# An attention and feed-forward kernel on one core: last product of a projection step behind the unit's values, output bias by column groups and added a unit later

## The chip, the core and the metric

The kernel runs on one core of a Trainium2 chip. The metric is the device time of one execution in microseconds (us). The time before is the median of three runs, 1138.49 us (1137.04 to 1140.65). The engines of a core work side by side, each through its own queue in order: TensorE (PE; its weight loads are shown as PEld), VectorE (DVE), ScalarE (ACT), GpSimd (POOL) and SyncE (SP, which here only issues transfers). Products land in PSUM, from which VectorE and ScalarE read.

## The reference

Four sequences of 1024 tokens with 512 features. First cross attention with 16 heads of 32 features (`_layernorm` subtracts the mean and divides by the deviation), then a feed-forward part whose inputs and weights are rounded to 8-bit steps:

```python
x = x + xattn(layernorm(x), ctx)       # 16 heads, mask below
x = x + ffn(layernorm(x))

# xattn
qh = heads(q @ Wq + bq);  kh = heads(kv @ Wk + bk);  vh = heads(kv @ Wv + bv)
scores = where(mask, qh @ kh.T / sqrt(32), -inf)
out = merge(softmax(scores) @ vh) @ Wo + bo
# mask: tokens 0..767 attend within their own third of 256;
#       tokens 768..1023 attend to 0..767 and causally to each other

# ffn; fq is a rounding to 8-bit steps with one scale for a whole tensor, fw with one for a row
h = fq(silu(fq(x) @ fw(w_gate).T) * (fq(x) @ fw(w_up).T))
return h @ fw(w_down).T
```

The biases bq, bk, bv and bo are not zero.

## The kernel before

The time falls into the attention part (to about 880 us), which this change touches, and the feed-forward part.

**Blocks and units.** Tokens come in 16 blocks of 256, four to a sequence. Three blocks of a sequence attend to their own keys only, the fourth (TEXT) to the keys of all four. A unit is one block of queries, one group of four heads (four groups) and one block of keys; there are 112 units. All products are 32-bit. The values, the sums and the projections go through `column_groups` or its like: four matmuls of 128 rows by 32 columns side by side. One such matmul instruction appears as two records in the trace.

**The loop over units** (lines 819 to 898) writes the order of TensorE, VectorE, ScalarE and GpSimd by hand (`manual_schedule`); SyncE's queue is ordered by the scheduler. A turn n does, in this order:

1. `maxima` of unit n: scores s, reduced on VectorE to row maxima.
2. Perhaps one step of a background task (statistics or normalisation of a block of x, rounding of a weight for the feed-forward part).
3. `large(n)`: one large step. This is a projection step (`big_step`, `run_big`: pp_kv or pp_q through `rows`, or pv) or a step of the output product (`step_output`, `Output.step`: po). A counter `spent` against `target(n)` paces the projections; `outputs` is the queue of finished blocks.
4. What `later` holds from the turn before: quotients of finished units, `add_bias`.
5. `weights` of unit n - 5: scores again, transposed, into t; ScalarE takes their exponentials into pT (two instructions of 128x1024); GpSimd adds these into sp for the softmax sums (L516).
6. `values` of unit n - 6: av, and, at the last key block of a group, the sums (L548, a product of ones with sp).
7. Where the projections are behind, a second large step.

**A projection step.** `rows` makes two halves of 256 columns (`parts`) in one PSUM tile. For each half it adds four products over the input chunks (`ci`); each product is one call of `column_groups`. After both halves ScalarE takes them out with bias and scale (line 286). A pv step fills 512 columns and ScalarE copies them out (line 326). For the last units, from `LATE` on, each step does one half only and has a PSUM tile of its own. A po step is taken out by VectorE, which adds it to xr (line 589).

**PSUM.** `ps_sc` holds three buffers of two banks for s and t; `ps_av` one bank for av; `ps_mm` one bank for all large steps, so each large step waits until the one before is taken out. Before the loop, `bank` uses `ps_sc` for them.

**The output bias.** bo + bv Wo is the same for all tokens. `output_bias` spreads bv over 128 columns (turn 2), multiplies it with Wo in four full matmuls (turn 4) and adds bo on VectorE. `Output.load` loads the block of x into xr; `add_bias` adds bo_b to it on GpSimd (line 584) in the turn after the load.

## Time and profile before

| | |
|---|---|
| median of three runs | 1138.49 us |
| profiled execution, its own time | 1139.15 us |
| its span, first to last instruction | 1137.4 us |
| mean granted TensorE clock | 0.992 |
| TensorE busy | 1116.0 us, 98% |
| VectorE, ScalarE, GpSimd busy | 784.9, 500.1, 551.5 us |
| attention's first part, 0 to 126 us: TensorE busy | 123.9 us |
| steady part, 126 to 740 us: TensorE busy | 612.2 of 614 us |
| late part, 740 to 880 us: TensorE busy | 135.8 of 140 us |

The page sums an engine's busy time over the whole span. A matmul's end in the trace is modelled, and a wait of TensorE shorter than that end isn't seen as idle: it shows in the distance from one start to the next. In a timeline, each row gives the start, the length, the engine, the line, what is written from what, and, in brackets, the idle time before it and what ended that.

### The profile page before, as it was taken

The numbers are of one execution on the slowest core, as the hardware profiler recorded it, in microseconds if no ns is written. First come the engines' busy times: TensorE is split into PE (matmuls) and PEld (weight loads), VectorE is DVE, ScalarE is ACT, GpSimd is POOL, SyncE is SP. The second block draws the span as 40 slices with busy tenths as digits, with TensorE's granted clock in tenths as the row PEclk, the third lists the DMA queues.
The fourth block names the chain that finished last, engine by engine and source line by source line (L and its number), as shares of the span: only waits on it lengthen the run. The fifth ranks groups of instructions, "written<-read, shape, count | busy, mean of one in ns | idle before, by whom it ended". The sixth has DMA issues, their size and how long they took to land.

```text
span 1137.4 us, 31369 instructions
## 1 busy us (share of the span) xinstructions
PE 1116.0 (98%) x13811; PEld 562.5 (49%) x13833; DVE 784.9 (69%) x979; ACT 500.1 (44%) x700; POOL 551.5 (48%) x618
## 2 busy tenths in 40 slices
PE   9999999999999999999999999998999899998998
PEld 5545545455545445454545455555554344444344
DVE  2545776766577857567777765875667788877887
ACT  3234433343444424344433445543333465553553
POOL 1224556577664567775556568657753222110110
PEclk9999999999999999999999999999999899999999
DMA  8342213133222222331312122111311599320895
GB/s 260 109 123 74 62 43 108 47 88 93 80 62 76 79 84 63 95 101 34 92 67 73 56 76 73 37 49 27 106 61 62 164 291 268 69 38 28 290 386 194
DMA packets 117201, 119.09 MB, mean 105 GB/s; under 512 B 55548, under 2 KB 86536, under 8 KB 115656
## 3 DMA queue, kind: packets, MB, share of 16 engines
q1 hardware_dynamic: 111104, 83.26, 26.3%
q0 software_dynamic: 5648, 33.30, 7.6%
q8 instruction: 108, 1.77, 0.7%
q10 hardware_dynamic: 312, 0.53, 0.2%
q14 instruction: 29, 0.24, 0.1%
HBM read 71.57 MB, written 33.29 MB: 92 GB/s over the span
## 4 chain that ended last, share of the span: by engine, by line
PE 91%; DVE 3%; DMA 2%; POOL 2%; ACT 1%; issue 1%; DVEq 0%; POOLq 0%; ACTq 0%
PE pv L219 10%; PE po L219 9%; PE pp_kv L219 9%; PE pp_q L219 9%; PE av L530 9%; PE t L491 8%; PE pg L1045 7%; PE pu L1045 7%; PE s L439 6%; PE s L428 5%; PE t L486 3%; PE av L548 3%; PE pd L1148 2%; DMA xt<-x_d 2%; POOL sp L516 2%
## 5 line engine op out<-in xcount | busy, mean ns | idle before, releaser
L496 ACT ACTIVATE pT<-t 128x1024 f32<-128x1024 f32 x224 | 217.1, 1021 | 190.2 <-PE t L491 160.1
L516 POOL TENSOR_TENSOR sp<-sp,pT 128x1024 f32<-128x1024 f32 x86 | 191.7, 2229 | 39.1 <-ACT pT L496 35.6
L450 DVE TENSOR_REDUCE nmh<-s 128x2 f32<-128x1024 f32 (+1 forms) x128 | 145.3, 1156 | 67.3 <-PE s L439 65.1
L516 POOL TENSOR_TENSOR sp<-pT 128x1024 f32<-128x1024 f32 x59 | 139.9, 2372 | 87.9 <-ACT pT L496 87.7
L432 DVE TENSOR_REDUCE nmh<-s 128x4 f32<-128x1024 f32 x96 | 112.8, 1216 | 97.7 <-PE s L428 95.5
L219 PE MATMUL pp_q<-qT,Wq_sb 128*32 128x256 f32 x2048 | 119.3, 383 | 0.0
L530 PE MATMUL av<-pT,va 128*32 128x256 f32 (+1 forms) x1792 | 116.5, 377 | 1.0 <-ACT avs L893 1.0
L219 PE MATMUL pv<-Wv_sb,kvT 128*32 128x512 f32 (+1 forms) x1088 | 116.9, 570 | 0.0
L491 PE MATMUL t<-qT,kT 32*128 32x256 f32 (+1 forms) x1792 | 113.4, 367 | 0.0
L219 PE MATMUL po<-Wo_sb,oT 128*32 128x512 f32 (+1 forms) x1120 | 110.3, 534 | 0.3
L563 DVE RECIPROCAL avs<-avs 128x256 f32<-128x256 f32 x63 | 109.8, 1742 | 0.0
L219 PE MATMUL pp_kv<-kvT,Wk_sb 128*32 128x256 f32 x1920 | 109.6, 380 | 0.0
L564 POOL TENSOR_TENSOR oT<-avs 128x256 f32<-128x256 f32 x63 | 45.9, 729 | 98.1 <-DVE avs L563 98.0
L491 PEld LDWEIGHTS t<-qT,kT 32*128 32x128 f32 x1792 | 88.3, 185 | 7.0
L1045 PE MATMUL pg<-xqT,wgT 128*128 128x512 bf16 x344 | 90.2, 382 | 1.1 <-DVE xqT L1006 0.5
L1045 PE MATMUL pu<-xqT,wuT 128*128 128x512 bf16 x345 | 90.2, 382 | 0.4
L1051 ACT ACTIVATE silu<-pg,sg 128x512 f32<-128x512 f32 x88 | 60.0, 686 | 65.6 <-PE pg L1045 63.5
L219 PEld LDWEIGHTS pp_q<-qT,Wq_sb 128*32 128x32 f32 x2048 | 63.7, 110 | 48.8 <-issue 8.7
L1072 DVE SCALAR_TENSOR_TENSOR h<-pu,su,silu 128x512 f32<-128x512 f32 x88 | 65.4, 747 | 30.9 <-PE pu L1045 28.3
L219 PEld LDWEIGHTS pp_kv<-kvT,Wk_sb 128*32 128x32 f32 x1920 | 60.1, 110 | 44.1 <-issue 5.4
L439 PE MATMUL s<-kT,qT 32*128 32x256 f32 (+1 forms) x1024 | 76.4, 387 | 3.2 <-ACT pT L496 3.2
L530 PEld LDWEIGHTS av<-pT,va 128*32 128x32 f32 x1792 | 46.8, 109 | 54.5 <-issue 23.7
(186 smaller groups left out, 1387.3 us busy)
## 6 DMA issues: line engine op xcount, KB each, us to landing
xt<-x_d SPq DMA_DIRECT2D x16, 1024.0 KB, 6.4
h<-h_d POOLq DMA_DIRECT2D x3, 2816.0 KB, 13.6
xb<-in_x_dram SPq DMA_DIRECT2D x16, 512.0 KB, 3.7
xr<-in_x_dram SPq DMA_DIRECT2D x16, 512.0 KB, 3.7
x_d<-xr POOLq DMA_DIRECT2D x16, 512.0 KB, 3.9
spread_kv<-in_ctx_dram SPq DMA_DIRECT2D x60, 128.0 KB, 2.7
xn_d<-xb SPq DMA_DIRECT2D x15, 512.0 KB, 3.3
spread_q<-xn_d SPq DMA_DIRECT2D x60, 128.0 KB, 2.7
```

What stands on the lines that cost most here:

```text
L219: nc.tensor.matmul(out[rows_of(j)], lhs[:, rows_of(j)], rhs, start=start, stop=stop, tile_position=(0, j * D), skip_group_check=True)
L432: nc.vector.tensor_reduce(nmh[:, h, :, :, 0], prs[h], AX.X, ALU.max, negate=True)
L439: nc.tensor.matmul(prs[j // 2][:, j % 2, kk, :w], q[rows_of(j), g, i * P : (i + 1) * P], K[k.keys[2 * half + kk]][rows_of(j), g, :w], star ...
L450: nc.vector.tensor_reduce(nmh[:, h, :, i, half], s[:, :, :n], AX.X, ALU.max, negate=True)
L491: nc.tensor.matmul(prs[j // 2][:, j % 2, n, cols], kc[rows_of(j), g, n * P : (n + 1) * P], q[rows_of(j), g, cols], start=False, stop=(n == 1))
L496: nc.scalar.activation(pT[:, 2 * h : 2 * h + 2], prs[h], AF.Exp)
L516: nc.gpsimd.tensor_tensor(sp[:, :, cols], a, pT[:, :, n, cols], ALU.add)
L530: nc.tensor.matmul(av[rows_of(j), 0, cols], va[:, n, g * P + j * D : g * P + (j + 1) * D], u.pT[:, j, n, cols], start=(u.part == 0 and n = ...
L563: nc.vector.reciprocal(avs[:, 1, :], avs[:, 1, :])
L1045: nc.tensor.matmul(ps, w[:, cc, ic * P : (ic + 1) * P], qT[:, cc, :], start=(cc == 0), stop=(cc == NCC - 1))
L1051: nc.scalar.activation(s, pg, AF.Silu, scale=sg[:, ic : ic + 1])
L1072: nc.vector.scalar_tensor_tensor(h[:, ic, :], pu, su[:, ic : ic + 1], s, ALU.mult, ALU.mult)
```

## The change

Three parts.

The last of the products of a large step is held back, with its take: `run_big` and `step` return them as two functions (`rest`), and `complete` runs them. In the loop, `complete` comes straight after the large step where the unit of values in this turn is the last of its group (sums follow), where there is none, where a second large step follows, or where these values need the very block that is being projected. Else it comes after `weights` and `values`. `rows` is rewritten for it: the take of a half now follows the last product of that half, and only the last half's last product and take are held back. In the changed kernel the take of `rows` is line 294.

`add_bias` passes through `later` twice, so it comes one turn later.

The output bias: bv stands in the first of 32 columns with zeros beside it; four matmuls of 128x32, each in its own group of 32 partitions, give four partial products; ScalarE copies them out; a turn later one product with ones adds them up.

```diff
         def output_bias():
-            bvr = wk2.tile([P, NCC, P], F32, tag="wst", name="bvr", bufs=1)
+            bvr = wk2.tile([P, NCC, D], F32, tag="wst", name="bvr", bufs=1)
+            parts = wk2.tile([P, C], F32, tag="sp", name="bo_parts")
             def spread():
-                nc.vector.tensor_copy(bvr, bqk[:, 2 * NCC :].unsqueeze(2).to_broadcast([P, NCC, P]))
+                nc.vector.memset(bvr, 0.0)
+                nc.vector.tensor_copy(bvr[:, :, 0:1], bqk[:, 2 * NCC :].unsqueeze(2))
             def product():
...
-                    nc.tensor.matmul(pb, bvr[:, cc, :], W["Wo"][:, cc, :], start=(cc == 0), stop=(cc == NCC - 1))
+                    nc.tensor.matmul(pb[rows_of(cc)], bvr[:, cc, :], W["Wo"][:, cc, :], start=True, stop=True, tile_position=(0, cc * D), skip_group_check=True)
+                nc.scalar.copy(parts, pb)
+            def total():
+                pb = ps_sc.tile(...)
+                nc.tensor.matmul(pb, ones, parts, start=True, stop=True)
                 nc.vector.tensor_tensor(bo_b, pb, bo_b, ALU.add)
...
             def rows(self, dst, w, b, scale, co, parts):
                 pk = bank(...)
-                for a in parts:
-                    for ci in range(NCC):
-                        lhs = W[w][:, ci, (co + a) * P : (co + a + 1) * P]
-                        column_groups(pk[:, a, :], lhs, self.T[:, ci, :], ci == 0, ci == NCC - 1)
-                for a in parts:
+                def product(a, ci):
+                    lhs = W[w][:, ci, (co + a) * P : (co + a + 1) * P]
+                    column_groups(pk[:, a, :], lhs, self.T[:, ci, :], ci == 0, ci == NCC - 1)
+                def take(a):
                     bias = bqk[:, b + co + a : b + co + a + 1]
                     nc.scalar.activation(dst[:, co + a, :], pk[:, a, :], AF.Identity, bias=bias, scale=scale)
+                todo = [(a, ci) for a in parts for ci in range(NCC)]
+                for a, ci in todo[:-1]:
+                    product(a, ci)
+                    if ci == NCC - 1:
+                        take(a)
+                return (lambda: product(*todo[-1])), (lambda: take(parts[-1]))
...
-                    later.append(self.add_bias)
+                    later.append(lambda: later.append(self.add_bias))
...
+        late_rest = []
+        def finish(rest, rests):
+            late_rest.extend(rest)
+            if not rests:
+                complete()
+        def complete():
+            for f in late_rest:
+                f()
+            late_rest.clear()
...
             full = large(n)
+            v = units[n - V_LAG] if V_LAG <= n < len(units) else None
+            second = n < LATE and spent + BIG < target(n)
+            if v is None or second or v.part == v.parts - 1 or (jobs[at_big - 1].kind, jobs[at_big - 1].c) == ("kv", v.k.keys[v.part]):
+                complete()
...
                 ends = values_now()
                 weights_now()
+            complete()
```

The pv step and `Output.step` are split in the same way: all products but the last at once, the last one and its take in `rest`. With the take of a block's last po step, the load of the next xr moves too. `large` passes `rests=True` to every step it makes; the other callers complete at once.

More of the change, by code (lines that the diff above doesn't have):

```diff
@@ L197, in product @@
                 for cc in range(NCC):
-                    nc.tensor.matmul(pb, bvr[:, cc, :], W["Wo"][:, cc, :], start=(cc == 0), stop=(cc == NCC - 1))
+                    nc.tensor.matmul(pb[rows_of(cc)], bvr[:, cc, :], W["Wo"][:, cc, :], start=True, stop=True, tile_position=(0, cc * D), skip_group_check=True)
+                nc.scalar.copy(parts, pb)
+            def total():
+                pb = ps_sc.tile([P, 2, 2, QB], F32, tag="sc", name="pbt").rearrange("p a b c -> p a (b c)")[:, 0, :]
+                nc.tensor.matmul(pb, ones, parts, start=True, stop=True)
                 nc.vector.tensor_tensor(bo_b, pb, bo_b, ALU.add)
-            return spread, product
+            return spread, product, total
         nc.gpsimd.memset(mask, 0.0)
@@ L312, in run_big @@
                         Q[c] = qp.tile([P, NCC, QB], F32, tag="qT", name=f"qT_{c}")
-                    self.rows(Q[c], "Wq", 0, QK_SCALE, 2 * i, parts)
+                    rest = self.rows(Q[c], "Wq", 0, QK_SCALE, 2 * i, parts)
                 elif i < 2:
@@ L316, in run_big @@
                         K[c] = kp.tile([P, NCC, QB], F32, tag="kT", name=f"kT_{c}")
-                    self.rows(K[c], "Wk", NCC, 1.0, 2 * i, parts)
+                    rest = self.rows(K[c], "Wk", NCC, 1.0, 2 * i, parts)
                 else:
@@ L323, in run_big, with product @@
                     pv = bank(f"pv_{c}_{i}_{parts[0]}")
-                    for ci in range(NCC):
+                    def product(ci):
                         column_groups(pv[:, cols], self.T[:, ci, i * P : (i + 1) * P], W["Wv"][:, ci, cols], ci == 0, ci == NCC - 1)
-                    nc.scalar.copy(V[c][:, i, cols], pv[:, cols])
+                    for ci in range(NCC - 1):
+                        product(ci)
+                    rest = (lambda: product(NCC - 1)), (lambda: nc.scalar.copy(V[c][:, i, cols], pv[:, cols]))
                 if parts[-1] == 1:
@@ L331, in run_big @@
                     self.part = 1
-                return len(parts)
+                return len(parts), rest
         background = deque()
@@ L608, in step, with product, take @@
                 po = ps_mm.tile([P, 512], F32, tag="mm", name=f"po_{self.k.n}_{i}_{self.part}")
-                for cc in range(NCC):
+                last = cols.stop == C
+                def product(cc):
                     column_groups(po[:, cols], self.k.oT[:, cc, i * P : (i + 1) * P], W["Wo"][:, cc, cols], cc == 0, cc == NCC - 1)
-                statistics = self.take(po, i, cols)
-                if statistics is None:
-                    self.part = 1
-                else:
-                    background.appendleft(statistics)
-                    self.part = 0
-                    self.i += 1
+                def take():
+                    statistics = self.take(po, i, cols)
+                    if last:
+                        background.appendleft(statistics)
+                for cc in range(NCC - 1):
+                    product(cc)
+                self.part = 0 if last else 1
+                self.i += last
+                return (lambda: product(NCC - 1)), take
         quantised = [False]
@@ L700, with big_step @@
         rows_done = {}
-        def big_step(half=False):
+        def big_step(half=False, rests=False):
             nonlocal at_big, spent
             j = jobs[at_big]
-            spent += BIG * j.run_big(half) / 2
+            parts, rest = j.run_big(half)
+            spent += BIG * parts / 2
             rows_done[j.kind[0], j.c] = min(2 * j.big + j.part, NCC)
@@ L709, in big_step @@
                 at_big += 1
+            finish(rest, rests)
+        late_rest = []
[7 more added lines that the diff above has]
+            late_rest.clear()
         def advance(n):
@@ L734, with step_output, take @@
         outputs = []
-        def step_output(half=False):
-            outputs[0].step(half)
+        def step_output(half=False, rests=False):
+            rest = outputs[0].step(half)
             if outputs[0].i == 2:
                 outputs.pop(0)
-                for o in outputs[:2]:
-                    o.load()
+                def take():
+                    rest[1]()
+                    for o in outputs[:2]:
+                        o.load()
+                finish((rest[0], take), rests)
+            else:
+                finish(rest, rests)
         def finished(k):
@@ L751, in large @@
                 if outputs and (len(outputs) > 1 or spent + BIG >= target(n)):
-                    step_output()
+                    step_output(rests=True)
                 elif can_big(n) and spent < target(n):
-                    big_step()
+                    big_step(rests=True)
                 elif outputs:
-                    step_output()
+                    step_output(rests=True)
                 elif can_big(n) and spent < target(n) + 3 * BIG:
-                    big_step()
+                    big_step(rests=True)
                 else:
@@ L761, in large @@
             elif can_big(n):
-                big_step(n < len(units))
+                big_step(n < len(units), True)
             elif outputs:
-                step_output(n < len(units))
+                step_output(n < len(units), True)
             else:
@@ L817 @@
         early[0] = False
-        spread, product = output_bias()
+        spread, product, total = output_bias()
         for n in range(len(units) + V_LAG):
@@ L829 @@
                     minus_maxima(u)
-            if n in (2, 3, 4):
-                (spread, sigmoids, product)[n - 2]()
+            if n in (2, 3, 4, 5):
+                (spread, sigmoids, product, total)[n - 2]()
             f = background.popleft() if background and n > 0 else None
```

## The prediction

> **What bounds the kernel now.** I read the page first, then the windows by stage, then timelines of single units.

> ```profile
> span 1137.4 us, 31369 instructions
> PE 1116.0 (98%) x13811; PEld 562.5 (49%) x13833; DVE 784.9 (69%) x979; ACT 500.1 (44%) x700; POOL 551.5 (48%) x618
> ```
> ```profile
> 126.00:740.00 614.00, 612.22 (x9068) 313.30 (x9060) 425.97 (x513) 268.07 (x392) 392.65 (x391) 1.00 0.25 73
> ```
> In the windows (columns: length, then busy PE, PEld, DVE, ACT, POOL, then clock) TensorE is busy for 612 of 614 us of the steady attention stage at full clock. So whatever is added to TensorE's stream there is added to the time; whatever lies on the other engines is hidden unless TensorE waits for it.

> TensorE's part of the timeline shows a unit: s (maxima), a large step (pp, pv or po), t (weights), av (values), sometimes a second large step.

> ```profile
> 406.49 1.15 PE L439 MATMUL s<-kT,qT 32*128 32x256 f32 x16
> 407.57 3.64 PE L219 MATMUL po<-Wo_sb,oT 128*32 128x512 f32 x32
> ...
> 436.56 1.07 PE L530 MATMUL av<-pT,va 128*32 128x256 f32 x16
> 437.56 1.38 PE L439 MATMUL s<-kT,qT 32*128 32x256 f32 x16
> 438.88 3.66 PE L219 MATMUL pp_q<-qT,Wq_sb 128*32 128x256 f32 x64
> ```
> The first s follows a second large step: next step 407.57 - 406.49 = 1.08 us after it began. The other follows av directly: 438.88 - 437.56 = 1.32. The missing 0.24 us is a wait hidden inside a "busy" row: s needs two of three score buffers, one of which still holds t until ScalarE's first exp has read it (437.65 to 438.67 is the second exp of that pair, so the first ends about when s begins). This is what the moved product can fill.

> How a bank is handed over, in ScalarE's timeline and that of the weight loads:

> ```profile
> 406.63 0.84 ACT L286 ACTIVATE kT<-pp_kv,bqk 128x256 f32<-128x256 f32 x2 [2.54 <-PE pp_kv L219]
> 407.57 0.16 PEld L219 LDWEIGHTS po<-Wo_sb,oT 128*32 128x32 f32 x8 [0.33 <-ACT kT L286]
> ```
> ```profile
> L286 ACT ACTIVATE kT<-pp_kv,bqk x60: 465/473/475, 35.5 to 722.5; 128x256 f32<-128x256 f32 x60
> ...
>   PE pp_kv L219: 88.3, 32
> ```
> One take of 128x256 lasts 0.47 us (two overlap to 0.84). It begins about 0.45 us after the last product's start (406.18 to 406.63), and TensorE restarts 0.1 us after it ends (407.47 to 407.57). ScalarE was idle for 88.3/32 = 2.8 us before such a take.

> **The change, part by part.** The sum is made against the profiled execution, 1139.15 us (span 1137.4 and 1.75 around it; 0.66 above the median 1138.49).

> *1. rows() now takes half 0 of a projection before half 1 is multiplied: +42.7 us, and +2.4 at the start.* The diff reads as if this only let ScalarE begin earlier. Both halves lie in one PSUM tile. In the built program of the changed kernel, the first matmul of half 1 carries a wait for ScalarE's take of half 0:

> ```
> L226 Matmult pp_kv_7_2_0<-kvT_7,Wk_sb 32x256 x16
> L226 Matmult pp_kv_7_2_0<-kvT_7,Wk_sb 32x256 [waits Activation]
> L226 Matmult pp_kv_7_2_0<-kvT_7,Wk_sb 32x256 x15
> ```
> Before, the 32 ran without a wait. I count 54 steps with two halves (28 pp_kv, 26 pp_q); the half steps near the end have a bank each. [...] By the rows alone the two halves are different columns, and a take of 0.47 us beside 1.7 us of products costs TensorE nothing; the sum is then 14.1 of gain, 1125. [...] No row of before shows it, since no take ran inside a step. [...] Price, from the hand-over above: 0.45 to ScalarE's start, 0.47 take, 0.07 to 0.1 to restart, 1.0 from the last start of half 0; without a wait they follow after 0.22 us (a pp step is 64 matmul records, 16 groups of four side by side, in the 3.59 us that the chain of waits shows for it). Stall 0.79, with 0.70 and 0.85 as ends (a 0.42 take and immediate restart; 24 ns more of refill). 54 x 0.79 = 42.7. ScalarE is free at each midpoint: the tightest case is the apply of the norm (L365), which ends 0.26 to 0.4 us before the take could start. The one exception is pp_q's second step at the start, where apply stands first and ends at 31.91 while half 0 is done near 29.9: some 2.4 us more. What waits behind TensorE here is everything, and no other engine is late enough for its own wait to shrink.

> *2. The last product (one of four input chunks) behind the values: -9.0 us.* In the built order 42 steps are split: 23 pp, 12 pv, 7 po. Nothing is added to TensorE; the product (0.43 us at 256 columns, 0.86 at 512) fills the 0.24 us wait of s. The mode sequence is unchanged, since av and the products are both 128*32. The new risk is the single ps_mm buffer: the take now stands behind both exps on ScalarE, and the next large step queues behind it. With s starting at 0 before, the first exp ends at 0.14 and the second at 1.05; a pp take then ends near 1.45 to 1.5, TensorE could go on at 1.55, and the next step wants the bank at 0.43 + 0.77 + 0.31 = 1.51. So pp loses 0.02 to 0.09 of its 0.24; pv wants the bank at 1.9 and its 0.59 us copy ends near 1.7; po is taken by VectorE. With a take of po go its store of x1 (GpSimd, 0.8 us to issue) and the next load of xr, by less than a unit; a landing takes 3.8 us and its first use is units away. 23 x 0.19 + 19 x 0.24 = 8.9, rounded to 9. Ends: 10 (no hand-over loss) and 2 (the bank late by 0.2 us at each pp and pv).

> *3. Output's bias add a unit later: -3.5 us.* GpSimd works in order, and at one place the add waits for the load of xr and holds the sums behind it:

> ```profile
> 770.71 2.38 POOL L584 TENSOR_TENSOR xr<-xr,bo_b 128x1024 f32<-128x1024 f32 x1 [9.25 <-DMA xr<-in_x_dram]
> 773.03 0.74 POOL L564 TENSOR_TENSOR oT<-avs 128x256 f32<-128x256 f32 x1
> 773.72 4.79 POOL L516 TENSOR_TENSOR sp<-sp,pT 128x1024 f32<-128x1024 f32 x2
> ...
> 778.54 1.94 ACT L496 ACTIVATE pT<-t 128x1024 f32<-128x1024 f32 x2 [4.18 <-POOL sp L516]
> 779.62 0.92 PE L439 MATMUL s<-kT,qT 32*128 32x256 f32 x12 [3.19 <-ACT pT L496]
> ```
> In the new order the pair of sums (4.8 us) and two short casts stand before that add; they start near 766 and end as the load lands, so exp isn't held. The other adds only change places within GpSimd's queue (48% busy); where the first product comes in the same unit, take() issues the add itself, at most 2.4 us before VectorE's turn, and the bank isn't wanted for longer than that. SP's queue moves a few xb, spread and transpose issues by one place, with units of slack. Ends: -3.8 and 0 (the wait moves to the next pair of sums).

> *4. Output bias in column groups: -1.6 us.*

> ```profile
> 57.79 3.70 PE L198 MATMUL pbo<-Wo_sb,bvr 128*128 128x512 f32 x8
> ```
> Eight full passes of 0.43 us become two grouped ones (four 128*32 matmuls side by side, as pv's rows run) and two full ones for total(): 3.43 - 1.72, less 0.1 for one more change of tiling (s to step costs 0.31 where the stream has 0.2). memset, the ScalarE copy (0.59 like pv's) and the later add lie beside the next steps; uncovered, they would cost about 1. Ends -2 and 0.

> Sum: 42.7 + 2.4 - 9.0 - 3.5 - 1.6 = +31.0; 1139.15 + 31.0 = 1170.2, or 1169.5 from the median. I say 1170.

> **Rivals.**
> *A: faster. The mid-step wait is covered*, because ScalarE's take finishes before TensorE would come to half 1. Then 1139.15 - 14.1 = 1125. For it: ScalarE is idle 2.8 us there. Against it: only 0.22 us separate the halves, the take alone lasts 0.47. It decides below (14.1 - 2.4)/54 = 0.22 us per wait. 5%.
> *B: the wait costs about half* (ScalarE starts sooner after a smaller group, 0.45 us each): 24.3 + 2.4 - 14.1 = +12.6, 1152. Against: the 0.45 us to ScalarE's start is the same in all 256-column takes. 7%.
> *C: the bank of the moved products is late as well*, and GpSimd's stall only moves: 2 in place of 9, 0 in place of 3.5: +41.5, 1181. For it: the take waits for two exps that end only 0.4 us before the bank is wanted. 12%.
> *D: the diff does not do what it says* (no split where it counts): excluded by the built order for the 42 moves; without their gain 1179, inside C.

> **How the numbers follow.** My forecast, 76%: 54 x 0.70 to 54 x 0.85 is 37.8 to 45.9, with 2.4 and gains of 10 to 16: 1163 to 1177. The range 1157 to 1180 adds the near halves of B and C and leaves out some 15%. About 0.3% (3.4 us) is what a measurement of this kernel can tell from no change. Of A's 5%, 1 falls inside that, where only part of the wait is covered: faster 0.04, same 0.01, slower 0.95.

> **What would show it.** In the changed profile: pp steps of two halves last 4.45 in place of 3.66 us, and before their second half TensorE shows an idle of about 0.6 us released by ScalarE's L294 (1.0 less the 0.38 that a product's record lasts); TensorE's busy share in the steady stage falls to about 96%; s after a moved product at 1.15; pbo gone from 3.70 to under 2; no 9 us wait at the add of xr, nor the 3.2 us one of s. If pp steps keep 3.66 us, I am wrong in the main term and A holds. If steps after moved products start with an idle on ScalarE, C does.

## The result, and the profile after

| | before | after |
|---|---|---|
| median of six runs, us | 1138.26 | 1176.14 |
| lowest to highest, us | 1137.04 to 1140.65 | 1174.14 to 1182.36 |
| profiled execution, us (span) | 1139.15 (1137.4) | 1178.07 (1176.3) |
| granted TensorE clock | 0.992 | 0.993 |

The changed kernel takes 1.0339 times as long, with a 95% interval of 1.0314 to 1.0365. It is slower, by about 38 us; 31 were forecast. In two of the experiments below some executions came out about 2% longer at a lower granted clock (1206.26 us at 0.986 in one, 1190.47 at 0.988 and 1198.96 at 0.984 in another), and times and ratios leave these out.

The page of the changed kernel, its span and the line of busy times:

```profile
span 1176.3 us, 31381 instructions
PE 1118.4 (95%) x13835; PEld 546.4 (46%) x13835; DVE 784.8 (67%) x980; ACT 502.6 (43%) x701; POOL 551.6 (47%) x618
```

TensorE is busy for 1118.4 us where it was busy for 1116.0: nearly the same work, in a span that is 38.9 us longer. The share fell from 98% to 95%, so what was added is idle time. The windows of the steady stage (length, then busy PE, PEld, DVE, ACT, POOL, clock) say the same:

```profile
126.00:770.00 644.00, 616.35 (x9084) 302.66 (x9080) 423.41 (x507) 267.97 (x390) 388.31 (x390) 1.00 0.25 70
```

616.35 of 644 us is 95.7%, at full clock; before it was 612.22 of 614. Who causes the idle time stands in TensorE's waits (waiter, releaser: total us, times, longest):

```profile
PE pp_q L226 <- ACT qT L294: 18.3, 29, 2.9
PE pp_kv L226 <- ACT kT L294: 16.6, 28, 0.6
PE po L226 <- DVE xr L608: 1.8, 2, 1.2
PE t L505 <- DVE nmh L469: 1.8, 3, 0.7
...
PE po_tail L828 <- POOL xr L603: 1.4, 1, 1.4
```

None of these stood among the long waits before. The first two are the projection steps waiting for ScalarE, 34.9 us together: 54 times for the take of their own first half (34.4), and three times, 0.18 us each, for the take of the moved step before. The other three are small, and none of them was in the prediction. TensorE's part of the timeline shows the step itself, and the held-back product:

```profile
421.07 1.07 PE L549 MATMUL av<-pT,va 128*32 128x256 f32 x16
421.96 0.61 PE L226 MATMUL pp_q<-qT,Wq_sb 128*32 128x256 f32 x8
422.50 1.15 PE L458 MATMUL s<-kT,qT 32*128 32x256 f32 x16
423.60 3.64 PE L226 MATMUL po<-Wo_sb,oT 128*32 128x512 f32 x32
...
429.25 1.91 PE L226 MATMUL pp_kv<-kvT,Wk_sb 128*32 128x256 f32 x32
431.75 1.93 PE L226 MATMUL pp_kv<-kvT,Wk_sb 128*32 128x256 f32 x32 [0.59 <-ACT kT L294]
433.62 1.15 PE L458 MATMUL s<-kT,qT 32*128 32x256 f32 x16
```

The pp_kv step is now two rows of 32 records. It takes 433.62 - 429.25 = 4.37 us to the next operation, 0.8 more than the 3.6 of an undivided one. Only 0.59 of it is printed as idle, because a record stays "busy" for 0.38 us after its start. Measured from start to start, the last group of half 0 and the first of half 1 are 0.99 us apart, where groups of one half follow after 0.22. In the upper half of the fence the held product of pp_q (8 records) stands between av and s, and s then needs 423.60 - 422.50 = 1.10 us, where the one that the prediction shows needed 1.32. So both mechanisms of the prediction are there, with the sizes it gave.

The stall of GpSimd is gone as well. Its timeline around the add of xr, now a unit later:

```profile
806.10 4.81 POOL L535 TENSOR_TENSOR sp<-sp,pT 128x1024 f32<-128x1024 f32 x2
...
811.87 2.37 POOL L603 TENSOR_TENSOR xr<-xr,bo_b 128x1024 f32<-128x1024 f32 x1
```

The pair of sums stands before the add, and the add has no wait in brackets, where 9.25 us stood. And the output bias, in TensorE's timeline:

```profile
66.11 1.06 PE L200 MATMUL pbo<-Wo_sb,bvr 128*32 128x512 f32 x8
...
76.69 1.13 PE L205 MATMUL pbt<-bo_parts,ones 128*128 128x512 f32 x2
```

3.70 us have become 1.06 and 1.13.

### The profile page after: what moved, and what is told of

Same layout as the page of the kernel before. It is cut to its first block, busy times and chain, and to the rows that moved or that the text cites. A ratio compares the mean times of both kernels' runs of the same rounds, so it can differ in the third digit from the quotient of the medians.

```text
span 1176.3 us, 31381 instructions
## 1 busy us (share of the span) xinstructions
PE 1118.4 (95%) x13835; PEld 546.4 (46%) x13835; DVE 784.8 (67%) x980; ACT 502.6 (43%) x701; POOL 551.6 (47%) x618
## 4 chain that ended last, share of the span: by engine, by line
PE 87%; DVE 4%; ACT 4%; DMA 2%; POOL 1%; issue 1%; DVEq 0%; POOLq 0%; ACTq 0%
PE pv L226 10%; PE pp_kv L226 10%; PE pp_q L226 9%; PE po L226 9%; PE av L549 8%; PE t L510 8%; PE pg L1097 7%; PE pu L1097 6%; PE s L458 5%; PE s L447 4%; PE t L505 3%; PE av L567 3%; PE pd L1200 2%; DMA xt<-x_d 2%; ACT pT L515 1%; ACT qT L294 1%
## 5 line engine op out<-in xcount | busy, mean ns | idle before, releaser
L535 POOL TENSOR_TENSOR sp<-sp,pT 128x1024 f32<-128x1024 f32 x86 | 191.6, 2228 | 42.6 <-ACT pT L515 39.1
L226 PE MATMUL pp_q<-qT,Wq_sb 128*32 128x256 f32 x2048 | 127.8, 384 | 18.4 <-ACT qT L294 18.3
L226 PE MATMUL pp_kv<-kvT,Wk_sb 128*32 128x256 f32 x1920 | 116.4, 382 | 17.3 <-ACT kT L294 16.6
L226 PE MATMUL pv<-Wv_sb,kvT 128*32 128x512 f32 (+1 forms) x1088 | 119.1, 570 | 0.0
L226 PE MATMUL po<-Wo_sb,oT 128*32 128x512 f32 (+1 forms) x1120 | 111.6, 534 | 1.8 <-DVE xr L608 1.8
L226 PEld LDWEIGHTS pp_q<-qT,Wq_sb 128*32 128x32 f32 x2048 | 61.0, 110 | 75.5 <-ACT qT L294 34.1
L583 POOL TENSOR_TENSOR oT<-avs 128x256 f32<-128x256 f32 x63 | 45.9, 729 | 105.7 <-DVE avs L582 105.7
L510 PEld LDWEIGHTS t<-qT,kT 32*128 32x128 f32 x1792 | 88.3, 184 | 6.6
L226 PEld LDWEIGHTS pp_kv<-kvT,Wk_sb 128*32 128x32 f32 x1920 | 57.3, 109 | 70.3 <-ACT kT L294 31.1
L458 PE MATMUL s<-kT,qT 32*128 32x256 f32 (+1 forms) x1024 | 70.4, 387 | 0.0
```

The costliest lines, as they stand in the source:

```text
L226: nc.tensor.matmul(out[rows_of(j)], lhs[:, rows_of(j)], rhs, start=start, stop=stop, tile_position=(0, j * D), skip_group_check=True)
L458: nc.tensor.matmul(prs[j // 2][:, j % 2, kk, :w], q[rows_of(j), g, i * P : (i + 1) * P], K[k.keys[2 * half + kk]][rows_of(j), g, :w], star ...
L510: nc.tensor.matmul(prs[j // 2][:, j % 2, n, cols], kc[rows_of(j), g, n * P : (n + 1) * P], q[rows_of(j), g, cols], start=False, stop=(n == 1))
L535: nc.gpsimd.tensor_tensor(sp[:, :, cols], a, pT[:, :, n, cols], ALU.add)
```

## The experiments

**One part of the change at a time.** Four kernels; the ratios are to the kernel before.

*The changed kernel without the take in mid-step.*

```diff
                 for a, ci in todo[:-1]:
                     product(a, ci)
-                    if ci == NCC - 1:
-                        take(a)
-                return (lambda: product(*todo[-1])), (lambda: take(parts[-1]))
+                return (lambda: product(*todo[-1])), (lambda: [take(a) for a in parts])
```

> The changed kernel, but in a projection step both halves are taken after the last product, as before the change; the rest of the change stays. Theory (the mid-step wait, 54 times 0.80 us and 2.3 at the start, is the loss): those 45.5 us come back, less 3 to 5 us because the moved steps of two halves now have two takes (0.84 us) behind the exps and their bank is late: 1132 to 1136 us. No row of L226 waits for L294 inside a step; pp steps last 3.66 us again. Rival (the loss comes from the held-back product, its late bank and the later takes): stays at 1165 us or more.

Measured: 1135.05 us, ratio 0.9974 (0.9964 to 0.9985). The 41 us come back, and the kernel is now a little faster than before. The price named in the expectation is visible too. The timeline of one moved pp_kv step, both takes behind the exps:

```profile
250.44 1.15 PE L445 MATMUL s<-kT,qT 32*128 32x256 f32 x16
251.00 0.84 ACT L294 ACTIVATE kT<-pp_kv,bqk 128x256 f32<-128x256 f32 x2
251.90 2.78 PE L226 MATMUL po<-Wo_sb,oT 128*32 128x512 f32 x24 [0.32 <-ACT kT L294]
```

The same unit in the changed kernel, where only one take is left for this place:

```profile
272.59 1.15 PE L447 MATMUL s<-kT,qT 32*128 32x256 f32 x16
273.16 0.48 ACT L294 ACTIVATE kT<-pp_kv,bqk 128x256 f32<-128x256 f32 x1
273.69 2.78 PE L226 MATMUL po<-Wo_sb,oT 128*32 128x512 f32 x24
```

Two takes last 0.84 us and one 0.48, and the next step, which needs the bank, starts 1.46 us after s instead of 1.10. In the 14 moved steps of two halves the move costs 0.14 to 0.36 us each with both takes at the end; with one take it gains 0.2 in most. So the early take has a use, but only in these 14 of the 54 steps of two halves.

*The kernel before, with the take in mid-step alone.*

```diff
-                for a in parts:
                     bias = bqk[:, b + co + a : b + co + a + 1]
                     nc.scalar.activation(dst[:, co + a, :], pk[:, a, :], AF.Identity, ...)
```

(The two loops over the halves become one.)

> The kernel before, with only this of the change: half 0 of a projection step is taken before half 1 is multiplied. Theory: 1138.3 + 54 x 0.80 + 2.4 to 3.5 at the start = 1184 to 1185 us; pp steps of two halves last 4.45 us, with waits for L294 of some 35 us in all. Rival (it is the wait together with the held-back product that costs, since the take stands behind fewer other things here): 1138 to 1160.

Measured: 1184.89 us, ratio 1.0415 (1.0397 to 1.0433). The take alone makes the whole loss and more. Its waits of TensorE:

```profile
PE pp_q L219 <- ACT qT L285: 17.7, 26, 2.9
PE pp_kv L219 <- ACT kT L285: 16.6, 28, 0.6
```

26 and 28 waits are the 54 steps of two halves, now without any product held back.

*The kernel before, with the add a unit later alone.*

```diff
-                    later.append(self.add_bias)
+                    later.append(lambda: later.append(self.add_bias))
```

> The kernel before, with only output's bias added one unit later. Theory from the two traces: the wait of GpSimd for one late load, and with it 5.3 us of waits of s and av, goes; the last block's add now delays the tail's first product, +2.1: 1138.3 - 5.3 + 2.1 = 1135.1 us, 1134.5 to 1136. Rival 1 (the stall only moves to the next pair of sums): 1138 to 1141. Rival 2 (the tail's wait has another cause): 1133.

Measured: 1135.37 us, ratio 0.9972 (0.9963 to 0.9980), which is 3.2 us less. In its trace the start of s in unit 102 is 5.25 us earlier than before, measured from unit 101. GpSimd's timeline there, and a line of TensorE's waits:

```profile
767.30 4.81 POOL L516 TENSOR_TENSOR sp<-sp,pT 128x1024 f32<-128x1024 f32 x2 [0.40 <-ACT pT L496]
...
773.08 2.36 POOL L584 TENSOR_TENSOR xr<-xr,bo_b 128x1024 f32<-128x1024 f32 x1
```
```profile
PE po_tail L782 <- POOL xr L584: 1.4, 1, 1.4
```

The stall doesn't move to the next sums, so the first rival falls. The second line is the cost: the last block's add now stands in front of the tail's first product. It is there without the other parts of the change, so it belongs to this one.

*The kernel before, with the output bias in column groups alone.*

```diff
-                    nc.tensor.matmul(pb, bvr[:, cc, :], W["Wo"][:, cc, :], ...)
+                    nc.tensor.matmul(pb[rows_of(cc)], bvr[:, cc, :], W["Wo"][:, cc, :], ..., tile_position=(0, cc * D), ...)
+                nc.scalar.copy(parts, pb)
+            def total(): ...
```

> The kernel before, with only output's bias in column groups (four zero-padded columns of 32, then one product with ones). Theory: the product of 3.1 us at L198 goes to 0.5, one product of 1.06 and a change of tiling are added, net -1.7: 1136.6 us. Rival (memset, copy and the later add aren't covered and hold the first units): 1138 to 1139.

Measured: 1136.0 us, ratio 0.9988 (0.9976 to 1.0000). The interval ends at no change, so the times alone hardly show it. The trace does: the next step follows 0.9 us after the product began, and by the starts of s over units 4 to 6 the edit gains 2.77 us in one unit and gives 1.06 back in the next.

```profile
57.66 1.06 PE L200 MATMUL pbo<-Wo_sb,bvr 128*32 128x512 f32 x8
58.55 7.09 PE L226 MATMUL pp_kv<-kvT,Wk_sb 128*32 128x256 f32 x128
```

By these ratios the three parts add up to 47.2 - 3.2 - 1.4 = 42.6 us. The change as a whole costs 38.6. What is left for the held-back product is some 4 us of gain. The intervals of these terms are 1 to 3 us either way, so this is rough; the next section has it from the trace.

**What makes TensorE wait: the bank, the tile or the take?** In five steps of two halves near the start (two before the loop and the second large step of some early turns), the projection uses the three large score buffers instead of the one small bank. There a half can have a place of its own.

*A tile for each half in those five steps.*

```diff
...
+                if early[0]:
+                    pks = [bank(f"{name}_{a}")[:, :QB] for a in parts]
+                else:
+                    pk = bank(name)
+                    pks = [pk[:, :QB], pk[:, QB:]]
...
```

> The changed kernel, but in the five steps of two halves that use the score pool at the start, each half has a tile of its own (other banks). The early takes stay. Theory (TensorE waits because take and products share a tile of one bank, not because ScalarE is slow or the take itself costs): in these five steps the halves follow after 0.22 us, the other 49 keep their 0.99; 4 x 0.8 and the 3 us at the start come back, 1176.1 - 6 = 1170, less well if the second tile is late itself. Rival (TensorE waits for the take whatever the bank): the five waits and 1176 stay.

Measured: 1168.55 and 1169.64 us, ratio 1.0269 (1.0245 to 1.0294). With the median of before from the same session, 1138.84, that is 1169.5. The expected 6 us come back, and 49 of the 54 waits in mid-step are left. TensorE's timeline at the start:

```profile
23.44 7.09 PE L226 MATMUL pp_q<-qT,Wq_sb 128*32 128x256 f32 x128
30.46 0.70 PE L452 MATMUL s<-kT,qT 32*128 32x256 f32 x4
32.08 1.13 PE L452 MATMUL s<-kT,qT 32*128 32x256 f32 x12 [0.92 <-ACT qT L299]
```

The two pp_q steps run in one piece, 128 records in 7.09 us without a wait, although ScalarE takes half 0 during them as in the changed kernel. What is late next is s, by 0.92 us: it needs what ScalarE takes last. So a take beside the products costs nothing by itself; it is the next product's having to follow it that costs.

*The two halves in two banks, but of one tile.*

```diff
...
+                if early[0]:
+                    pk = ps_sc.tile([P, 2, 2, QB], F32, tag="sc", name=name)[:, :, 0, :]
...
```

> As the version in which the five early steps give each half a tile of its own, but the halves lie in the two banks of one tile of the score pool. If TensorE waits because two engines would meet in one bank, the five waits go as they did with two tiles: about 1169.5 us. If it waits because the program keeps product and take of one tile apart wherever they lie, the five waits of 0.6 us and more stay: about 1176.

Measured: 1176.58 us, ratio 1.0323 (1.0303 to 1.0342). Nothing comes back. Its timeline at the start:

```profile
23.54 1.91 PE L226 MATMUL pp_q<-qT,Wq_sb 128*32 128x256 f32 x32
26.04 3.66 PE L226 MATMUL pp_q<-qT,Wq_sb 128*32 128x256 f32 x64 [0.59 <-ACT qT L298]
32.60 1.93 PE L226 MATMUL pp_q<-qT,Wq_sb 128*32 128x256 f32 x32 [2.89 <-ACT qT L298]
```

0.59 and 2.89 us, as with one bank. In this program the wait is set by the tile: a product into a tile comes after a take of that tile that was issued before it, even where they are in different banks. Whether two tiles inside one bank would also wait is not shown.

**What is left of the held-back product.** Three kernels, each on top of the one before it.

*Half 0 taken early only where the last product is held back.* There the only product of the step still to come is the held one, three operations later. (`take_once` takes a half if it has not been taken yet.)

```diff
...
+                if len(parts) == 2:
+                    first_half.append(lambda: take_once(0))
...
                 complete()
+            for g in first_half:
+                g()
```

> The changed kernel, with half 0 of a projection step taken after the last product where that product isn't held back, and after the seventh product, beside t and av, where it is (14 steps). Theory: against the version with both takes at the end (1135) the 14 moved steps of two halves go from +0.15 to 0.36 us of loss to -0.22 of gain, some 5 us: 1130 us, with s to next step 0.30 again. Rival (the take ahead of the exps delays them, so s waits again): 1134 to 1137.

Measured: 1130.6 us, ratio 0.9928 (0.9913 to 0.9944). The timeline of the unit that was shown twice above:

```profile
250.43 1.15 PE L455 MATMUL s<-kT,qT 32*128 32x256 f32 x16
250.99 0.48 ACT L295 ACTIVATE kT<-pp_kv,bqk 128x256 f32<-128x256 f32 x1
251.52 2.78 PE L227 MATMUL po<-Wo_sb,oT 128*32 128x512 f32 x24
```

s to the next step is 1.09 us again. Split takes gain 4 to 5 us over two takes at the end, and no step waits in its middle.

*Products held back only before the last 28 units.*

```diff
-            if v is None or second or v.part == v.parts - 1 or ...:
+            if v is None or n >= LATE or second or v.part == v.parts - 1 or ...:
                 complete()
```

> As the version with half 0 taken early for held products alone, and products held back only before the last 28 units (n < LATE). Theory from the trace of the changed kernel: there the short steps before t expose VectorE's reduction (3.7 us of waits of t), a bank of po is late (0.7) and one take of po is queued behind statistics (1.05), against 2.6 us that the moves there gain: 2.9 us come back, 1127 us. Rival (those waits are there without the moves too): the 2.6 of gain is lost, 1132 to 1133.

Measured: 1127.81 us, ratio 0.9906 (0.9890 to 0.9922). Sixteen moves fewer (26 in place of 42) make the kernel 2.8 us faster by the medians; from the start of unit 84 to the last s the trace shows 2.1. In the last 28 units the moves cost more than they bring.

*The last block's bias added at once.*

```diff
+                    if self.k is units[-1].k:
+                        later.append(self.add_bias)
+                    else:
                         later.append(lambda: later.append(self.add_bias))
```

> As the version with products held back only before the last 28 units, and the last block's bias added in the unit of its load, the others a unit later. Theory: the tail's first product no longer waits for GpSimd's add: -2.1 us, 1125 us, no row of po_tail released by L603. Rival (the wait moves to the last sums or the quotient): 1127.

Measured: 1125.73 us, ratio 0.9883 (0.9866 to 0.9900). From the last s to the product pm_x (L112), the first that follows the attention part, the trace has 51.10 us, where the version without this edit has 52.62 and the kernel before 50.53. So 1.5 of the 2.1 us come back there, and 0.6 stay. The tail's first product has no wait:

```profile
859.80 1.13 PE L840 MATMUL po_tail<-xr,ident 128*128 128x512 f32 x2
```

This version is some 13 us faster than the kernel before and 50 faster than the changed one.

## Why the prediction was right, and where its terms were off

The direction, the cause and the range held (1157 to 1180; 1176 measured). The forecast of 1170 was 6 us low. Step 1 carries it; in step 2 a cost that nobody priced took half of the gain, and the net, -3.9, lies within that step's ends (10 and 2) by luck. Against its own steps, in us, from the starts of s in the two traces:

| step of the prediction | forecast | trace |
|---|---|---|
| 1. wait in mid-step, 54 steps | +42.7 | +43.2 |
| 1. more at the start | +2.4 | +3.5 |
| 2. held-back product (two places counted in the rows below) | -9.0 | -8.0 |
| 2. new waits made by the moves | not priced | +4.1 |
| 3. add a unit later, the stall | -3.5 | -5.3 |
| 3. add a unit later, the tail | not priced | +2.1 |
| 4. output bias | -1.6 | -1.7 |
| small differences of s in other units | | -0.8 |
| sum, up to pm_x | +31.0 | +37.1 (measured 37.6) |

The last 1.3 us, from there to the end of the span, lie in a part where no instruction differs. The version with both takes at the end differs by 1.1 us the other way in that part, so this is what two executions differ by.

*Step 1 was right in mechanism and size.* Half 1 follows 0.99 us after half 0, where 1.0 was worked out from 0.45 + 0.47 and the restart, in each of 53 steps within 3 ns; less 0.22, and with 0.02 because the second group after the wait comes 0.24 us after the first and not 0.22, that is 0.80 a step. That TensorE waits there stood in the built order; no row of before showed it, nor what causes it. The experiments do, for this program: with two banks in one tile it waits 0.59 us, as with one bank, and with two tiles it does not wait.

```profile
30.12:33.53 3.41, 0.74 (x16) 0.48 (x20) 0.00 (x0) 1.88 (x3) 2.35 (x6) 1.00 0.24 67
33.53:36.94 3.41, 3.41 (x36) 1.81 (x32) 0.00 (x0) 0.47 (x1) 0.00 (x0) 0.50 0.45 164
```
```profile
28.26:31.68 3.42, 1.44 (x28) 0.62 (x20) 0.00 (x0) 1.66 (x5) 2.48 (x9) 1.00 0.02 5
31.68:35.09 3.41, 2.49 (x44) 1.55 (x48) 0.00 (x0) 1.34 (x3) 0.76 (x2) 1.00 0.48 154
```
```profile
32.79 2.98 PE L226 MATMUL pp_q<-qT,Wq_sb 128*32 128x256 f32 x32 [2.89 <-ACT qT L294]
35.71 1.73 PE L447 MATMUL s<-kT,qT 32*128 32x256 f32 x16
```

In the changed kernel 2.67 us of one stretch are idle, and the next runs at a granted clock of 0.50: half a step takes 2.98 us, where 1.93 is usual, and the s takes 1.73 in place of 1.15. That is 1.6 us more than the waits explain; some 0.5 comes back at the s of the third unit, which had slack. In the kernel with two banks in one tile the border of the two stretches shown falls inside the same wait of 2.89 us: 1.98 us of one are idle and 0.92 of the next, the clock stays at 1.00, and the half step takes 1.93. How much idle time it takes is not shown: in the feed-forward part a stretch of the changed kernel with 1.79 us idle was followed by the half clock. The prediction named neither stretch nor clock.

*Step 2's gain per place was right, and its list of costs was short.* pv and po gain 0.24 to 0.26 each, pp mostly 0.22. In four units, where s is shorter (0.67 us in place of 0.77), the bank comes late by about what the move gains, and it is worth nothing. The term that failed is "the new risk is the single ps_mm buffer". The risk lies elsewhere: with a product less, t follows the start of a half step after 1.44 us instead of 1.87, and that product was what covered VectorE's reduction of s. The rows of such a unit in the changed kernel:

```profile
718.35 1.50 PE L226 MATMUL pp_q<-qT,Wq_sb 128*32 128x256 f32 x24
719.46 2.31 DVE L451 TENSOR_REDUCE nmh<-s 128x4 f32<-128x1024 f32 x2
719.79 0.39 PE L505 MATMUL t<-nmT,onesb 2*128 2x512 bf16 x2
720.70 0.39 PE L505 MATMUL t<-nmT,onesb 2*128 2x512 bf16 x2 [0.52 <-DVE nmh L451]
```

t needs a second score buffer, which VectorE is still reducing when the 24 records of pp_q are done. Six units have this: their t lasts 3.3 us longer in all than one without a wait, where the same units of the kernel before had 0.4. Some 0.9 comes back at one av, which waits 0.6 us for its sums where it waited 1.5. Two more places add 1.8 us. In one a pp_kv step wants the bank of a moved po 0.7 us before it is free. In the other VectorE, which works in order, has a unit's statistics ahead of the take of po:

```profile
849.20 0.64 DVE L615 BATCH_NORM_STATS2 st<-xr 128x6 f32<-128x512 f32 x1
...
851.13 0.42 DVE L608 TENSOR_TENSOR xr<-po,xr 128x256 f32<-128x256 f32 x1
...
851.60 1.50 PE L226 MATMUL po<-Wo_sb,oT 128*32 128x256 f32 x24 [1.23 <-DVE xr L608]
```

That makes some 3.8 us, all after unit 83; the 4.1 of the table are counted by the starts of s, and how much of them belongs to the gain of the row above is good to a few tenths. In the kernel that holds nothing back there the six waits are down to 0.6 us, those of the two places are gone, and it is faster by 2.8 us. So it is shown that holding back in these units costs more than it brings; the division among the three kinds of wait is read from the trace alone.

*Step 3 was mis-sized on both sides.* The stall was priced by the wait of s (3.2 us, and some 0.3 of restart). That was right for the wait, but a lower clock followed the idle time of 3.2 us (776.43 to 779.62). In the kernel before, two stretches of 3.41 us, the first with 2.05 us idle, and the half step that runs in the second:

```profile
777.57:780.98 3.41, 1.36 (x24) 1.04 (x28) 0.49 (x2) 1.94 (x2) 3.33 (x5) 1.00 0.10 19
780.98:784.39 3.41, 3.41 (x36) 1.64 (x32) 2.20 (x3) 0.47 (x1) 3.33 (x3) 0.50 0.21 43
```
```profile
780.47 3.20 PE L219 MATMUL pp_q<-qT,Wq_sb 128*32 128x256 f32 x32
```

3.20 us in place of 1.93, and the t after it takes 1.56 us to the next product, where the one before the wait took 0.98. So 5.3 us came back with the stall. The row of s that the prediction shows ends before the slow stretch begins, and the windows it used stop at 740. And "the other adds only change places within GpSimd's queue" missed the last one, which has no later unit to lie in:

```profile
907.35 2.38 POOL L603 TENSOR_TENSOR xr<-xr,bo_b 128x1024 f32<-128x1024 f32 x1
...
909.78 1.12 PE L828 MATMUL po_tail<-xr,ident 128*128 128x512 f32 x2 [1.44 <-POOL xr L603]
```

The kernel with only this part has the wait, and the one with the last add at once does not have it.

*Step 4 held*, at -1.7 in both traces that have it.

*The rivals.* A (covered wait) is excluded: each of the 54 waits is there, and removing them gives back 41 us. B (half price) is excluded by 0.80 us each. C (the bank late at moved steps, 1181) is nearest by its time, but for another reason: where a take is alone behind the exps the bank is late by 0.02 to 0.25 us, no more. The version with two takes there is what C describes, and it costs 14 moved steps 0.14 to 0.36 us each. The forecast was low because the misses on the slow side (0.5, 1.1, 4.1 and 2.1, and 1.0 of gain that didn't come) outweigh those on the fast side (1.8, 0.8 and 0.1).

## What to carry to other kernels

A take moved forward only overlaps with products if the program lets the next product go: find out which instruction waits for it, and price a hand-over there and back (here 0.99 us instead of 0.22) times the number of steps. If a piece of a step is moved to fill one wait, ask what the piece was covering where it stood. If work is put off by one round, look at the last round first; and price an idle time of TensorE of 3 us with the slower clock that can follow it (1.6 us at the start of the changed kernel, nothing in the kernel with two banks in one tile).
